# Host-laid taps and biases, an early load, a peeled last attention pair, and other memory for tiles of the triangle

## The chip, the cores and the metric

The kernel runs on one core of a Trainium2 chip, as one program. A core has TensorE (PE: matrix products into PSUM), VectorE (DVE), ScalarE (ACT), GpSimd (POOL) and SyncE (SP), each with its own stream of instructions, and 16 DMA engines that move data between DRAM and the on-chip memory (SBUF). The streams wait for each other by semaphores. The metric is the time of an execution on the device in microseconds (us), the median of several. Inputs may be laid out anew on the host; arithmetic on them is done by the kernel.

## The reference

An image x of 256 x 256 pixels by 128 channels in 32-bit floats passes through four layers. Each adds its output to x, and each begins with a normalisation over 32 groups of channels (`_gn`).

```python
# layer 0: row-wise attention, 4 heads of 32
zn = layernorm(gn(x)); q, k, v = zn @ Wq, zn @ Wk, zn @ Wv
a = softmax(q k^T / sqrt(32) + zn @ Wb)
x = x + (sigmoid(zn @ Wg) * (a @ v)) @ Wo
# layer 1: 16 steps of a gated complex recurrence, h <- f * (A h) + inp
A, B = fft2(pad(7x7 taps)), with A scaled below 0.95
f = sigmoid(u @ Wf + bf + 2); inp = 0.1 softplus(u @ Wd + bd) * sigmoid(u @ Wi + bi) * (B u)
x = x + h16
# layer 2: triangle product
p = layernorm(gn(x)); left, right = sigmoid(p @ g_in) * (p @ p_in), halves
out = einsum('bikd,bjkd->bijd', left, right / L)
x = x + sigmoid(p @ g_out) * (layernorm(out) @ p_out)
# layer 3: 3x3 convolution with bias, then a 128x128 product
x = x + (conv(gn(x), kernel) + bias) @ W
```

## The kernel before

The program runs six stages, one after the other, and passes the image between them through DRAM. For most work of TensorE, VectorE and ScalarE the order is the order of the code (`keep_in_program_order`, often behind a short name `pin`). For the rest, above all for where a load stands in its queue, a scheduler decides. Tiles come from pools; a tile in a pool waits until the earlier user of the same slot (or, for a pool that is closed and whose memory is used again, of the same bytes) is done. SP issues the loads, one after the other: a load that must wait holds all that are queued behind it. GpSimd issues the stores and does a little arithmetic. The very first weights are loaded from ScalarE's queue.

1. *Statistics* (`statistics`, about 0 to 134 us). Sums for the first normalisation over 32 chunks of 1 MB of x: VectorE subtracts a shift (`xs`, L220), ScalarE squares, TensorE adds up. The last seven chunks stay in SBUF. Beside this, `attention_weights` (L274) loads the weights of the attention, the block matrix `m32` as the last of them, and `bounded` (L470) computes a bound for the scores; its VectorE operations stand ahead of the first `xs`, among them one that multiplies by `m32` (L492). `kernel_rows` (L165) brings the 7 x 7 taps into two tiles of 21 x 64 x 32 (`ka0`, `ka1`): two memsets (L176) and eight loads (L178), all on GpSimd. TensorE makes 16 row transforms from them, and GpSimd stores these in the DRAM tensor `HD_`.
2. *Layernorm and transposition* (`attention`, to about 455 us), over the same 32 chunks. At chunk 5 `later_weights` (L312) queues the weights of the later layers on SP, among them three biases of the recurrence, each by two loads.
3. *Attention* (`attend_bounded`, 465 to 1707 us), 128 pairs of rows, about 9.6 us each. For one pair: scores into PSUM (`sc`, two buffers of two banks), bias added (`e`, VectorE), exponential (ScalarE), the two key halves added up (`ks`, `fold`), 48 matmuls for numerators and denominators (`nd`, one buffer of two banks, `values`), then `dn` (`gated`), its inverse on ScalarE (`inverse`), the quotient `og` (`divide`), the product with `Wo` (`px`) and the residual `x` (`output`), and squares for the next normalisation. The inverse, quotient and output of a pair are done in the turn of the next pair; after the loop the last pair's follow.
4. *Recurrence* (`recurrence`, to 3239 us), 64 blocks. `load(0)` fetches, with the block of x, the row transforms `hs` of that block from `HD_` by eight small loads; TensorE makes the column transform `za` from it.
5. *Triangle* (`triangle`, L1049). First part: 32 chunks are normalised (`zc`, `zs`, `zn`) and stored in `znT`; the load of `xin` (L1119) runs two chunks ahead, and `zn` has three buffers in the pool "t1". Second part, four quarters of the channels: 128 steps of `z` from `zt` (a load of 1 MB at L1169 for every two steps; `zt` has five slots in the pool `zp`, which is open from the beginning of the first part), gate `sg`, product into `LR`; then 32 steps of `po`, scaled and stored to `prodD`. `prepare` (`transformed_taps`, L1284) then transforms the taps of the convolution: `kw` and helpers in the pool "cwt", ending on VectorE at L1318. Last part: 32 steps with `pe` from `zn`, `zc` from the product `pr`, the layernorm and the output product `py`; loads of `zn`, `pr` and `xin` at L1213.
6. *Convolution* (`convolution`, to the end), untouched by the diff.

Of the kernel before, what the change touches and what calls it, by code (L numbers as in the profile page):

```python
# [9 lines left out]
F32 = mybir.dt.float32  # L10
# [7 lines left out]
P = 128  # L18
N = 256
# [3 lines left out]
KS = 7  # L23
HC = P // 2
# [6 lines left out]
class Kernel:  # L31
# [133 lines left out]
    def kernel_rows(self, sp, ps, HD_):  # L165

        nc, I = self.nc, self.i
        CG = HC // 4  # L170
        tu = self.load(sp, I["c_rows"], "tu")
        H, ka = [], []
        for n, (re, im) in enumerate((("A_real", "A_imag"), ("B_real", "B_imag"))):
            kr, ki = (I["L1_conv_" + y].rearrange("c p q -> p c q") for y in (re, im))
            k = sp.tile([3 * KS, HC, 32], F32, name=f"ka{n}")
            nc.gpsimd.memset(k, 0.0)  # L176
            for p0, q0, src in ((0, 0, kr), (0, KS, ki), (KS, 0, ki), (2 * KS, KS, kr)):
                nc.gpsimd.dma_start(k[p0:p0 + KS, :, q0:q0 + KS], src)  # L178
            ka.append(k)

        pin = lambda f: lambda *a, **k: self.tc.keep_in_program_order(f(*a, **k))

        def spectrum(g):
            n, g0 = divmod(2 * g, CG)
            if not g0:
                H.append(sp.tile([P, N, CG], F32, name="H", bufs=2))
            ph = ps.tile([P, 2, N], F32, name="ph", bufs=2)
            for j in range(2):
                for k in range(4):
                    pin(self.mm)(ph[32 * k:32 * k + 32, j], ka[n][:, CG * k + g0 + j, :], tu)  # L190
            pin(nc.scalar.copy)(H[n][:, :, g0:g0 + 2].rearrange("q u c -> q c u"), ph)
            if g0 + 2 == CG:
                for k in range(4):
                    nc.gpsimd.dma_start(HD_[n, :, k], H[n][32 * k:32 * k + 2 * KS])
        return spectrum
# [116 lines left out]
    def later_weights(self, pool):  # L312

        nc, I = self.nc, self.i
        W = self.weights = {}
        for g in "fid":
            W["W" + g] = self.load(pool, I["L1_conv_W" + g], "rw" + g)
            W["b" + g] = pool.tile([P, 2], F32, name="rb" + g)
            for half in range(2):
                with nc.allow_non_contiguous_dma("a bias vector"):  # L320
                    nc.sync.dma_start(W["b" + g][half * HC:(half + 1) * HC], I["L1_conv_b" + g].rearrange("(r c) -> c r", c=HC))

        W["ev"] = pool.tile([P, 2 * N], F32, name="ev")
        for o in range(0, P, 32):
            nc.sync.dma_start(W["ev"][o:o + 2 * KS], I["c_cols"])
        for n in ("in_w", "in_b", "out_w", "out_b"):
            W[n] = self.column(pool, I["L2_conv_ln_" + n], "ln2" + n)
        for n, src in (("p", "L2_p_in"), ("g", "L2_g_in"), ("o", "L2_p_out"), ("e", "L2_g_out"), ("kt", "L3_kernel"), ("wd", "L3_conv_W")):
            W[n] = self.load(pool, I[src], "w2" + n)
        W["bv"] = self.column(pool, I["L3_conv_bias"], "bv")  # L330

    def attention(self, wp, later, xT, x1T, znT, biasD, HD_, stats1, shift1):
        nc, tc, I = self.nc, self.tc, self.i
# [4 lines left out]
        with ExitStack() as c:  # L338
# [103 lines left out]
            for m in range(NM):  # L442
                turn(m + 1)
                variance(m)
                centre(m + 1, 0)
                normalise(m)
                pair_bias(m - 1)
                centre(m + 1, 1)
                if m == 5:
                    self.later_weights(later)  # L450
                elif m == NM - 4:
                    load_bias(0, 192)
                    nc.sync.dma_start(first[0], znT[:, :1024])
                    nc.sync.dma_start(first[1], xT[:, :1024])
                elif m == NM - 1:
                    load_bias(192, 240)
# [79 lines left out]
    def attend_bounded(self, xT, x1T, znT, bias, first, w, wo, stats1, shift1):  # L536


        nc, tc = self.nc, self.tc
        V = nc.vector  # L540
        with ExitStack() as c:
# [86 lines left out]
            def values(rp):  # L628

                v = t[rp, "v"]  # L630
                nd[rp] = ps.tile([P, 2, 2, N], F32, name="nd", bufs=1)
                for r in range(2):
                    i = 2 * rp + r
                    for kc in range(2):
                        for h in range(NH):
                            hs = slice(h * HD, (h + 1) * HD)
                            mm(nd[rp][hs, r, 0], v[:, 2 * r + kc, hs], es[i][:, h, kc], start=kc == 0, stop=kc == 1)
                    for h in range(NH):
                        mm(nd[rp][h * HD:(h + 1) * HD, r, 1], ones, ks[i][:, h])
# [51 lines left out]
            for i in range(2):  # L691
                score(i)
                for p2 in range(2):
                    biased(i, p2)
                    exponent(i, p2)
            for rp in range(N // 2):
                a, b = 2 * rp, 2 * rp + 1
                score(a + 2)
                inverse(rp - 1)
                biased(a + 2, 0)  # L700
                biased(a + 2, 1)
                divide(rp - 1)
                for nm in "qkvg":
                    if nm == "g":
                        exponent(a + 2, 0)
                    project(rp + 2, nm)
                fold(a)
                fold(b)
                output(rp - 1)
                score(b + 2)  # L710
                exponent(a + 2, 1)
                squares(rp - 1)
                for p2 in range(2):
                    biased(b + 2, p2)
                    exponent(b + 2, p2)
                values(rp)
                gated(rp)
            inverse(N // 2 - 1)
            divide(N // 2 - 1)
            output(N // 2 - 1)  # L720
            squares(N // 2 - 1)

    def attend_any(self, xT, x1T, znT, bias, w, wo, stats1, shift1):

# [88 lines left out]
    def recurrence(self, x1T, x2T, HD_, stats1, shift1, stats2, shift2):  # L813
# [7 lines left out]
        with ExitStack() as c:  # L821
# [44 lines left out]
            def load(b):  # L866
                d = D[b]
                xf = d["xf"] = io.tile([P, 1024], F32, name="xf", bufs=4)
                nc.sync.dma_start(xf, x1T[:, b * 1024:(b + 1) * 1024])
                xc = d["xc"] = io.tile([P, 2, 512], F32, name="xc")  # L870
                for half in range(2):
                    src = x1T[:, b * 1024 + half * 512:b * 1024 + (half + 1) * 512]
                    nc.sync.dma_start(xc[half * HC:(half + 1) * HC], src.rearrange("(r c) n -> c r n", c=HC))
                hs = d["hs"] = io.tile([P, 2, HC], F32, name="hs")
                for n in range(2):
                    for r in range(2):
                        o = 64 * n + 32 * r
                        for j in range(2):
                            nc.sync.dma_start(hs[o:o + 2 * KS, j].rearrange("q (k c) -> q k c", k=4),
                                              HD_[n, :, :, b * 4 + r + 2 * j, :])  # L880

# [165 lines left out]
    def triangle(self, x2T, x3T, znT, prodD, stats2, shift2, stats3, prepare):  # L1049
# [12 lines left out]
        with ExitStack() as c:  # L1062
# [47 lines left out]
            with ExitStack() as c1:  # L1110
# [31 lines left out]
                for m in range(NB // 2):  # L1142
                    load(m + 2)
                    centre(m + 1, 0)
                    rs = variance(ps, work, [sq[m, b] for b in range(2)])
                    square(m + 1, 0)
                    centre(m + 1, 1)
                    square(m + 1, 1)
                    pr = spreads(ps, rs)
                    zn = io.tile([P, 2048], F32, name="zn")  # L1150
                    for b in range(2):
                        z = zn[:, b * 1024:(b + 1) * 1024]
                        tt(z, zs[m, b], pr[b], MUL)
                        nc.gpsimd.tensor_scalar(z, z, lnw, lnb, MUL, ADD)
                    nc.gpsimd.dma_start(znT[:, m * 2048:(m + 1) * 2048], zn)

            with ExitStack() as c1:
# [6 lines left out]
                for g in range(G):  # L1164

                    for b in range(NB):
                        if b % 2 == 0:
                            zt = zp.tile([P, 2048], F32, name="zt")
                            nc.sync.dma_start(zt, znT[:, b * 1024:(b + 2) * 1024])  # L1169
                        z = ps.tile([P, 8, P], F32, name="z", bufs=3)  # L1170
                        for ch in range(8):
# [112 lines left out]
    def transformed_taps(self, late, kt, wd, bv):  # L1284
# [7 lines left out]
        MUL, ADD, SUB = ALU.mult, ALU.add, ALU.subtract  # L1292
        with ExitStack() as c:
            ps = c.enter_context(self.pool(name="cwp", bufs=2, space=PSUM))
            wt = c.enter_context(self.pool(name="cwt", bufs=1))
            pb = ps.tile([P, 2], F32, name="cpb")
            self.mm(pb[:, 0:1], wd, bv)
            V.tensor_copy(bw, pb[:, 0:1])
# [225 lines left out]
def arrays_of(inputs):  # L1524


    arrays = constants()
    for name, a in inputs.items():
        a = np.asarray(a)
        if name in _RENAMED:  # L1530
            if name == "L3_conv_kernel":
                a = a.reshape(9, P, P).transpose(2, 0, 1)
            else:
                a = a.T
            name = _RENAMED[name]
        arrays[name] = np.ascontiguousarray(a)
    return arrays


# [14 lines left out]
```

## Time and profile before

| what | us |
|---|---|
| three runs: median (lowest, highest) | 5127.24 (5122.95, 5130.06) |
| profiled execution | 5126.96 |
| its span | 5125.2 |
| busy: TensorE, VectorE, ScalarE, GpSimd | 4948.5, 4100.7, 3496.2, 414.2 |
| idle of TensorE ahead of the first `pe` of the triangle's last part | 9.82 |
| start of the first `xs` | 23.20 |
| last `og` and `x` of the attention | 1703.46, 1706.33 |

The times in the lower rows count from the start of the span. The profiled execution's own time is 1.8 us more than its span, which begins with the first and ends with the last recorded instruction. A line of a timeline or of a group of instructions is read so: start, busy time, engine, line of the kernel, operation, output <- inputs, shape, count, and in brackets the engine's idle time before it, with what ended it. "L60" is the line of the helper that issues every matmul and "L54" that of ScalarE's operations, so that these are told apart by the names of tiles. Waits of a DMA load appear where it stands in its queue (SPq). The granted clock of TensorE was 0.988 on average.

### The profile page before, as it was taken

What the parts mean: (1) busy time and instruction counts of PE and PEld (TensorE: products, weight loads), DVE (VectorE), ACT (ScalarE), POOL (GpSimd) and SP (SyncE); (2) the same over time, 40 slices, a digit from 0 to 9 for tenths busy, and PEclk for the clock granted to TensorE, in tenths of its full rate; (3) what the DMA queues carried; (4) which work ended last, traced back from release to release, by engine and by line L of the source; (5) the groups of instructions that cost most, each with busy time, mean ns of one, the idle gap of its engine ahead of it and who ended that gap; (6) DMA issues with size and microseconds to landing.
All of it is one profiled execution on the core that took longest, in us unless ns stands there. A gap on an engine that the chain in (4) does not pass through costs nothing.

```text
span 5125.2 us, 78589 instructions
## 1 busy us (share of the span) xinstructions
PE 4948.5 (97%) x31357; PEld 2702.7 (53%) x31357; DVE 4100.7 (80%) x4797; ACT 3496.2 (68%) x4948; POOL 414.2 (8%) x600
## 2 busy tenths in 40 slices
PE   7999999999999899999999999899999989989999
PEld 2444555555555333333333333229999953349999
DVE  6666999999999799999999999675333537779886
ACT  5445888888888799999999999453333357762110
POOL 1332000000000000000000000240111010000000
PEclk9999999999999899999999999999999999999999
DMA  8794222222222122222222222687666678865432
GB/s 282 277 338 186 83 79 87 83 80 87 83 80 82 59 76 63 76 63 76 63 76 63 76 63 67 253 304 280 239 229 238 237 277 325 327 224 188 140 121 67
DMA packets 205054, 781.44 MB, mean 152 GB/s; under 512 B 56857, under 2 KB 60263, under 8 KB 155423
## 3 DMA queue, kind: packets, MB, share of 16 engines
q1 hardware_dynamic: 147070, 505.57, 29.3%
q0 software_dynamic: 56320, 270.42, 14.5%
q8 instruction: 250, 4.10, 0.3%
q14 instruction: 118, 0.96, 0.1%
q10 hardware_dynamic: 1296, 0.40, 0.0%
HBM read 504.94 MB, written 271.32 MB: 151 GB/s over the span
## 4 chain that ended last, share of the span: by engine, by line
PE 56%; DVE 28%; issue 5%; ACT 1%; DMA 1%; POOL 0%; POOLq 0%; DVEq 0%; SPq 0%; ACTq 0%
PE z L60 9%; PE m L60 7%; PE nd L60 7%; PE sc L60 5%; PE po L60 4%; PE zc L60 4%; DVE tr L896 3%; DVE t L893 3%; DVE y L893 3%; DVE p L893 3%; DVE yf L893 3%; PE ppq L60 3%; PE ppv L60 2%; PE px L60 2%; PE pe L60 2%
## 5 line engine op out<-in xcount | busy, mean ns | idle before, releaser
L559 DVE TENSOR_TENSOR e<-sc,bT 128x1024 f32<-128x1024 f32 x512 | 603.2, 1220 | 52.4 <-PE sc L60 51.2
L54 ACT ACTIVATE e<-e 128x1024 f32<-128x1024 f32 x512 | 540.5, 1056 | 63.0 <-DVE e L559 49.2
L1056 DVE TENSOR_TENSOR LR<-z,sg 128x512 f32<-128x512 f32 x256 | 268.2, 1049 | 365.0 <-ACT sg L54 365.0
L60 PE MATMUL m<-U,v 128*128 128x128 f32 x4608 | 517.6, 276 | 6.6 <-DVE v L1403 6.6
L60 PEld LDWEIGHTS m<-U,v 128*128 128x128 f32 x4608 | 517.4, 193 | 6.7 <-DVE v L1403 6.7
L60 PE MATMUL z<-wf,zt 128*128 128x128 f32 x4096 | 460.4, 276 | 2.1 <-DVE zn L1056 1.3
L60 PEld LDWEIGHTS z<-wf,zt 128*128 128x128 f32 x4096 | 460.0, 193 | 3.9 <-DVE zn L1056 2.8
L54 ACT ACTIVATE sg<-z 128x512 f32<-128x512 f32 x256 | 152.8, 597 | 309.9 <-PE z L60 308.0
L54 ACT ACTIVATE sq<-zs 128x1024 f32<-128x1024 f32 x192 | 202.4, 1054 | 196.4 <-DVE zs L370 156.8
L559 DVE TENSOR_TENSOR ks<-e 128x1024 f32<-128x1024 f32 x256 | 300.9, 1217 | 0.0
L60 PE MATMUL sc<-tq,tk 32*128 32x256 f32 x4096 | 298.2, 403 | 2.8 <-DVE e L559 1.9
L60 PE MATMUL nd<-e,tv 128*32 128x256 f32 x4096 | 272.0, 383 | 0.0
L60 PEld LDWEIGHTS sc<-tq,tk 32*128 32x128 f32 x4096 | 187.3, 185 | 160.5 <-issue 97.1
L54 ACT ACTIVATE dn<-dn 128x512 f32<-128x512 f32 x384 | 241.7, 629 | 13.3 <-DVE dn L559 2.6
L60 PE MATMUL av<-y,ident 128*128 128x512 f32 x384 | 191.3, 607 | 44.9 <-DVE y L893 44.9
L60 PE MATMUL po<-LR 128*128 128x256 f32 x1024 | 222.2, 380 | 6.9 <-DVE LR L1056 6.9
L1440 ACT COPY m4s<-m 128x512 f32<-128x512 f32 x32 | 18.7, 584 | 287.8 <-PE m L60 287.8
L60 PEld LDWEIGHTS po<-LR 128*128 128x128 f32 x1024 | 194.1, 190 | 34.2 <-DVE LR L1056 7.7
L60 PE MATMUL bx<-p,ident 128*128 128x512 f32 x384 | 193.3, 612 | 0.0
L54 ACT ACTIVATE o<-po 128x256 f32<-128x256 f32 x256 | 84.3, 381 | 145.4 <-issue 110.5
L60 PEld LDWEIGHTS nd<-e,tv 128*32 128x32 f32 x4096 | 120.3, 110 | 109.8 <-issue 44.2
L862 ACT ACT_TABLE_LOAD x132 | 169.4, 1283 | 1.6
(368 smaller groups left out, 10276.9 us busy)
## 6 DMA issues: line engine op xcount, KB each, us to landing
zt<-znT SPq DMA_DIRECT2D x128, 1024.0 KB
znT<-zn POOLq DMA_DIRECT2D x64, 1024.0 KB, 5.3
xin<-x2T SPq DMA_DIRECT2D x64, 1024.0 KB
xin<-in_x_dram SPq DMA_DIRECT2D x50, 1024.0 KB
xr<-x3T SPq DMA_DIRECT2D x46, 768.0 KB
xT<-xo POOLq DMA_DIRECT2D x32, 1024.0 KB, 9.2
xr<-xT SPq DMA_DIRECT2D x64, 512.0 KB
zn<-znT SPq DMA_DIRECT2D x64, 512.0 KB
```

What stands on the lines that cost most here:

```text
L54: return self.nc.scalar.activation(out, in_, func, bias=bias, scale=scale, **kw)
L60: return self.nc.tensor.matmul(out, lhsT, rhs, start=start, stop=stop)
L559: pin = lambda f: lambda *a, **k: tc.keep_in_program_order(f(*a, **k))
L862: pin(nc.scalar.preload_act_table_set(want))
L893: pin(V.tensor_tensor(out, a, b_, op))
L896: pin(V.scalar_tensor_tensor(out, a, k, b_, op0, op1))
L1056: pin = lambda f: lambda *a, **k: tc.keep_in_program_order(f(*a, **k))
L1440: nc.scalar.copy(m4, m[4])
```

## The change

The taps are put into the shape of the tiles `ka0` and `ka1` on the host, with the zeros, and the biases as 128 x 2; each is then one load. The eight loads of row transforms become a method, `row_transforms`; block 0 calls it at chunk 12 of the layernorm, into a tile of its own in the pool `later`. In the attention the last pair is taken out of the loop: its `nd` takes a slot of `sc`, and its matmuls stand ahead of the quotient and output of the pair before. In the triangle the first part's `zn` comes from `zp`, under the same five slots as `zt`. The pool "cwt" is allocated at the other end of SBUF.

```diff
@@ -170,12 +170,9 @@
         CG = HC // 4
         tu = self.load(sp, I["c_rows"], "tu")
         H, ka = [], []
-        for n, (re, im) in enumerate((("A_real", "A_imag"), ("B_real", "B_imag"))):
-            kr, ki = (I["L1_conv_" + y].rearrange("c p q -> p c q") for y in (re, im))
+        for n in range(2):
             k = sp.tile([3 * KS, HC, 32], F32, name=f"ka{n}")
-            nc.gpsimd.memset(k, 0.0)
-            for p0, q0, src in ((0, 0, kr), (0, KS, ki), (KS, 0, ki), (2 * KS, KS, kr)):
-                nc.gpsimd.dma_start(k[p0:p0 + KS, :, q0:q0 + KS], src)
+            nc.gpsimd.dma_start(k, I["L1_taps"][n])
             ka.append(k)
 
         pin = lambda f: lambda *a, **k: self.tc.keep_in_program_order(f(*a, **k))
@@ -315,10 +312,7 @@
         W = self.weights = {}
         for g in "fid":
             W["W" + g] = self.load(pool, I["L1_conv_W" + g], "rw" + g)
-            W["b" + g] = pool.tile([P, 2], F32, name="rb" + g)
-            for half in range(2):
-                with nc.allow_non_contiguous_dma("a bias vector"):
-                    nc.sync.dma_start(W["b" + g][half * HC:(half + 1) * HC], I["L1_conv_b" + g].rearrange("(r c) -> c r", c=HC))
+            W["b" + g] = self.load(pool, I["L1_b" + g], "rb" + g)
 
         W["ev"] = pool.tile([P, 2 * N], F32, name="ev")
         for o in range(0, P, 32):
@@ -328,6 +322,16 @@
         for n, src in (("p", "L2_p_in"), ("g", "L2_g_in"), ("o", "L2_p_out"), ("e", "L2_g_out"), ("kt", "L3_kernel"), ("wd", "L3_conv_W")):
             W[n] = self.load(pool, I[src], "w2" + n)
         W["bv"] = self.column(pool, I["L3_conv_bias"], "bv")
+
+    def row_transforms(self, t, HD_, b):
+
+        for n in range(2):
+            for r in range(2):
+                o = 64 * n + 32 * r
+                for j in range(2):
+                    self.nc.sync.dma_start(t[o:o + 2 * KS, j].rearrange("q (k c) -> q k c", k=4),
+                                           HD_[n, :, :, b * 4 + r + 2 * j, :])
+        return t
 
     def attention(self, wp, later, xT, x1T, znT, biasD, HD_, stats1, shift1):
         nc, tc, I = self.nc, self.tc, self.i
@@ -448,6 +452,8 @@
                 centre(m + 1, 1)
                 if m == 5:
                     self.later_weights(later)
+                elif m == 12:
+                    self.first_rows = self.row_transforms(later.tile([P, 2, HC], F32, name="hs0"), HD_, 0)
                 elif m == NM - 4:
                     load_bias(0, 192)
                     nc.sync.dma_start(first[0], znT[:, :1024])
@@ -628,7 +634,7 @@
             def values(rp):
 
                 v = t[rp, "v"]
-                nd[rp] = ps.tile([P, 2, 2, N], F32, name="nd", bufs=1)
+                nd[rp] = ps.tile([P, 2, 2, N], F32, name="nd", **({"tag": "sc"} if rp == N // 2 - 1 else {"bufs": 1}))
                 for r in range(2):
                     i = 2 * rp + r
                     for kc in range(2):
@@ -693,7 +699,7 @@
                 for p2 in range(2):
                     biased(i, p2)
                     exponent(i, p2)
-            for rp in range(N // 2):
+            for rp in range(N // 2 - 1):
                 a, b = 2 * rp, 2 * rp + 1
                 score(a + 2)
                 inverse(rp - 1)
@@ -715,10 +721,20 @@
                     exponent(b + 2, p2)
                 values(rp)
                 gated(rp)
-            inverse(N // 2 - 1)
-            divide(N // 2 - 1)
-            output(N // 2 - 1)
-            squares(N // 2 - 1)
+
+            rp = N // 2 - 1
+            inverse(rp - 1)
+            fold(N - 2)
+            fold(N - 1)
+            divide(rp - 1)
+            values(rp)
+            gated(rp)
+            output(rp - 1)
+            inverse(rp)
+            squares(rp - 1)
+            divide(rp)
+            output(rp)
+            squares(rp)
 
     def attend_any(self, xT, x1T, znT, bias, w, wo, stats1, shift1):
 
@@ -871,13 +887,7 @@
                 for half in range(2):
                     src = x1T[:, b * 1024 + half * 512:b * 1024 + (half + 1) * 512]
                     nc.sync.dma_start(xc[half * HC:(half + 1) * HC], src.rearrange("(r c) n -> c r n", c=HC))
-                hs = d["hs"] = io.tile([P, 2, HC], F32, name="hs")
-                for n in range(2):
-                    for r in range(2):
-                        o = 64 * n + 32 * r
-                        for j in range(2):
-                            nc.sync.dma_start(hs[o:o + 2 * KS, j].rearrange("q (k c) -> q k c", k=4),
-                                              HD_[n, :, :, b * 4 + r + 2 * j, :])
+                d["hs"] = self.first_rows if b == 0 else self.row_transforms(io.tile([P, 2, HC], F32, name="hs"), HD_, b)
 
 
 
@@ -1147,7 +1157,7 @@
                     centre(m + 1, 1)
                     square(m + 1, 1)
                     pr = spreads(ps, rs)
-                    zn = io.tile([P, 2048], F32, name="zn")
+                    zn = zp.tile([P, 2048], F32, name="zn", tag="zt")
                     for b in range(2):
                         z = zn[:, b * 1024:(b + 1) * 1024]
                         tt(z, zs[m, b], pr[b], MUL)
@@ -1165,7 +1175,7 @@
 
                     for b in range(NB):
                         if b % 2 == 0:
-                            zt = zp.tile([P, 2048], F32, name="zt")
+                            zt = zp.tile([P, 2048], F32, name="zt", tag="zt")
                             nc.sync.dma_start(zt, znT[:, b * 1024:(b + 2) * 1024])
                         z = ps.tile([P, 8, P], F32, name="z", bufs=3)
                         for ch in range(8):
@@ -1292,7 +1302,7 @@
         MUL, ADD, SUB = ALU.mult, ALU.add, ALU.subtract
         with ExitStack() as c:
             ps = c.enter_context(self.pool(name="cwp", bufs=2, space=PSUM))
-            wt = c.enter_context(self.pool(name="cwt", bufs=1))
+            wt = c.enter_context(self.pool(name="cwt", bufs=1, side="right"))
             pb = ps.tile([P, 2], F32, name="cpb")
             self.mm(pb[:, 0:1], wd, bv)
             V.tensor_copy(bw, pb[:, 0:1])
@@ -1534,6 +1544,16 @@
                 a = a.T
             name = _RENAMED[name]
         arrays[name] = np.ascontiguousarray(a)
+
+
+    taps = np.zeros((2, 3 * KS, HC, 32), np.float32)
+    for n, m in enumerate("AB"):
+        re, im = (arrays.pop(f"L1_conv_{m}_{y}").transpose(1, 0, 2) for y in ("real", "imag"))
+        for p0, q0, a in ((0, 0, re), (0, KS, im), (KS, 0, im), (2 * KS, KS, re)):
+            taps[n, p0:p0 + KS, :, q0:q0 + KS] = a
+    arrays["L1_taps"] = taps
+    for g in "fid":
+        arrays["L1_b" + g] = np.ascontiguousarray(np.tile(arrays.pop("L1_conv_b" + g).reshape(2, HC).T, (2, 1)))
     return arrays
```

## The prediction

> **What bounds the kernel now.** I read the page's engine and chain parts first, to learn who carries the end, and then five places in the trace where the edits act: the timeline of VectorE at the start, the windows of DMA traffic, TensorE's timeline at the end of the attention, the chain of work through the normalisation of the triangle, and the timelines at its two later borders.
>
> ```profile
> PE 4948.5 (97%) x31357; PEld 2702.7 (53%) x31357; DVE 4100.7 (80%) x4797; ACT 3496.2 (68%) x4948; POOL 414.2 (8%) x600
> ...
> PE 56%; DVE 28%; issue 5%; ACT 1%; DMA 1%; POOL 0%; POOLq 0%; DVEq 0%; SPq 0%; ACTq 0%
> ```
>
> TensorE is busy 97% of the span, and the chain that ends last runs on TensorE and VectorE. The edits remove no instruction from either, so they can win only idle time at a border. DMA is 1% of the chain, about 51 us; the question is which of these microseconds go.
>
> The start, VectorE's timeline (start, duration, instruction, idle before and its releaser):
>
> ```profile
> 15.91 0.23 DVE L300 TENSOR_SCALAR woh<-wo 128x128 f32<-128x128 f32 x1 [5.69 <-DMA wo<-in_L_conv_Wo_dram]
> ...
> 18.14 0.28 DVE L497 TENSOR_REDUCE sums<-jq 128x1 f32<-128x128 f32 x1
> 22.79 0.29 DVE L492 TENSOR_TENSOR junk<-junk,m 128x128 f32<-128x128 f32 x1 [4.37 <-DMA m<-in_c_block_dram]
> ...
> 23.20 2.35 DVE L220 TENSOR_TENSOR xs<-xin,sh 128x1024 f32<-128x1024 f32 x2
> ```
>
> The first chunk's `xs` stands behind `junk` (L492), which waits for the block matrix m32 to 22.79. The first chunk of x had landed long before. m32 was issued at 5.40 and `wo` at 4.91, both on ScalarE's queue; a weight issued at 3.58 landed 2.26 us later. The windows show why they took 10 and 17 us (columns: window, its length, busy time of PE, PEld, DVE, ACT, POOL, then granted clock, DMA share, GB/s):
>
> ```profile
> 5.00:10.00 5.00, 2.89 (x12) 2.32 (x12) 2.63 (x15) 1.28 (x1) 5.00 (x7) 1.00 0.96 248
> 10.00:15.00 5.00, 1.14 (x4) 0.84 (x4) 0.22 (x2) 0.00 (x0) 0.96 (x2) 1.00 1.15 141
> 15.00:20.00 5.00, 1.77 (x6) 1.43 (x6) 1.87 (x9) 0.00 (x0) 0.00 (x0) 1.00 1.01 95
> ```
>
> ```profile
> 4165.00:4185.00 20.00, 16.96 (x54) 6.00 (x53) 6.33 (x6) 14.62 (x16) 0.00 (x0) 1.00 1.01 419
> ```
>
> From 10 to 20 us the DMA engines are as full as at 4165, but move 95 to 141 GB/s instead of 419. In this time GpSimd's eight tap loads are in flight (issued 4.24 to 10.16, the last landing at 24.1), 12.2 KB each in runs of 7 floats.
>
> The end of the attention, TensorE's timeline:
>
> ```profile
> 1695.84 1.33 PE L60 MATMUL px<-og,wo 128*128 128x512 f32 x2 [2.88 <-DVE og L559]
> 1697.09 1.94 PE L60 MATMUL nd<-e,tv 128*32 128x256 f32 x16
> ...
> 1700.71 0.60 PE L60 MATMUL nd<-ks,ones 128*32 128x256 f32 x8
> 1704.21 2.08 PE L60 MATMUL px<-og,wo 128*128 128x512 f32 x2 [2.89 <-DVE og L559]
> ```
>
> `nd` of the last pair begins only after `og` of the pair before has read the one `nd` buffer.
>
> The triangle's normalisation, chain of work:
>
> ```profile
> 3286.26 8.95 DMA znT<-zn
> 3295.23 0.33 SPq L1169
> 3295.66 15.46 DMA xin<-x2T
> ```
>
> A store of zn holds a zt load (L1169) at SP's head, and the xin load queued behind it comes late. Chunks that otherwise start every 6.33 us then start at 3301.27, 3310.68 and 3317.42: 9.41 + 6.74 − 2 × 6.33 = 3.49 us lost.
>
> Border to the quarters (VectorE), then border to the last stage (the chain, then TensorE's timeline):
>
> ```profile
> 3464.45 2.81 DVE L1056 TENSOR_TENSOR LR<-z,sg 128x512 f32<-128x512 f32 x3 [6.19 <-ACT sg L54]
> ```
>
> ```profile
> 4153.63 0.48 DVE U L1318
> ...
> 4154.16 4.91 DMA zn<-znT
> ```
>
> ```profile
> 4147.83 1.55 PE L60 MATMUL cpk<-w2wd,w2kt 128*128 128x128 f32 x11
> 4159.20 6.28 PE L60 MATMUL pe<-zn,w2e 128*128 128x512 f32 x8 [9.82 <-DMA zn<-znT]
> ```
>
> LR is first written at 3464.45, although its `sg` was ready at 3461.61: the memory is that of the last zn, whose store landed at 3464.08. The last stage's first zn lies over kw, so its load leaves only when L1318 is done, and TensorE idles 9.82 us.
>
> **What the Trainium skill says.** "DMA: Bandwidth & Descriptors", section Specifications: line rate wants transfers of at least 512 B. The trace agrees in direction (28 B runs, 95 to 141 GB/s). The same page, "Issuing engines are not separate DMA queues": transfers of SP, ScalarE and GpSimd run on the same 16 engines and interleave; agreed, since the taps stretch ScalarE's 64 KB load from 2.26 to 17 us. "TensorE: Matmul & The Clock Gate", "What's actually happening": an idle window of about 3.4 us halves the clock; agreed, `pe` takes 6.28 us after 9.82 idle and 3.63 afterwards.
>
> **Part by part.**
>
> *Taps (A).* Removed: two memsets (3.54 us of GpSimd) and eight loads; added: two loads of 172 KB in 8 KB runs, issued near 1 us. The 246 KB more cost about 1.0 us at 248 GB/s. With the slow traffic gone, x's first two chunks at 360 GB/s (the rate around 8 us) are in by about 12, and `wo` and m32 between them by about 10 to 11.5. From `wo`'s first use to L492 being ready to run are 18.42 − 15.91 = 2.5 us, so the first `xs` starts near 13.2 against 23.20: gain 10.0. Ends: 13 if everything lands in 2.3 us (then the first chunk, landed 10.69, decides), 2.5 if x's own traffic is what delays m32. I take 10: the slow packets begin and end with the taps. From the first `xs` the stage goes as before (TensorE fills 25 to 30 us), so the gain travels.
>
> *Biases and early hs (B).* On SP three loads for six, and eight hs loads moved from the recurrence's first block to the layernorm, in two lots of four between later weights and chunks of x. The eight took 1707.76 to 1715.05, 7.3 us of SP's queue; the chunks behind them are needed 40 us later or more, which hides it. In the recurrence TensorE goes from zd straight to za at 1717.11 without waiting for hs: gain 0. Without that cover it would cost 7.3.
>
> *Last pair (C).* nd in a scores' buffer starts when its last e exists, 1693.0. The two `ks` move ahead of og(126) and end at 1696.05. nd's 48 matmuls end near 1696.9; then dn 0.7, ScalarE 2 × 0.64, x(126) 0.7 in between, og 0.65, px 1.33 from 1699.7 (2.08 if cold), x at about 1701.5 against 1706.33. og(126) and px(126) go behind nd, where TensorE would otherwise idle; ScalarE's squares(126) goes behind the last inverse, and nobody waits for it. Gain 4.8 (4.4 to 5.3).
>
> *zn in zt's slots (D).* The five early zt loads leave their places among the xin loads, so SP no longer stalls on a store: gain 3.5 (3 to 4). The price: zt 0 to 3 now wait for the stores of zn 27 to 30, landing 3439.5 to 3458.5, and land about 5 us later; they are needed at 3457.2 and each 3.57 us from about 3463. All come ahead by my count, the closest by 2 to 3 us.
>
> *LR free of zn (E).* LR can start at 3461.6, 2.8 earlier. But TensorE runs z ahead in three PSUM buffers and idles only 0.76 at 3464.77: gain 0.8 (0 to 2).
>
> *kw elsewhere (F).* zn(0) and most of pr(0) load during the quarters' po matmuls. `pe` then waits for bwc alone (done 4150.56): 4150.6 to 4154.2 at 3.63 warm. The last rows of pr follow the last product's store (issued 4148.03), landing near 4153. So zc(0) starts at about 4154.3 against 4165.49: gain 11.2. Limit: from 4165 to 4185 the DMA runs at 419 GB/s; pr(1) would land near 4160.8 and is needed at 4164. If that slips, the gain is 8, at worst 7; at best 13.
>
> Sum: 10.0 + 0 + 4.8 + 3.5 + 0.8 + 11.2 = 30.3. The profiled execution took 5126.96 us (span 5125.2, the rest lies around it), 0.3 below the median of 5127.24: 5096.7, or 5097 on the median.
>
> **Rivals.**
>
> *Start bound by x itself.* Five chunks of 1 MB go out before 30 us and could fill the engines without any taps. For: at 5 to 10 us the share is 0.96. Against: that is at 248 GB/s and the slow time starts with the taps. A is 2.5, the time 5104.5.
>
> *Last stage fed by DMA.* For: shares of 0.90 to 1.01 from 4165 to 4225. Against: TensorE has no idle there from 4185. F is 8 or 7: 5100 to 5101.
>
> *Slower: first quarter starved.* Before, five zt stand ready when z starts; after, the quarter begins with one or two, and four of the five slots turn over at first. A slot gives four periods of 3.57 us = 14.3 us from release to landing. It decides from 4.5 us per MB (233 GB/s): 32 loads × 0.93 = 30 us, the whole gain; at 5 us per MB it costs 46: 5143. Against: other quarters hold 1 MB per 3.57 us (293 GB/s) with the same five slots, and VectorE's normalisation is over by then.
>
> *Hardly any change.* The same mechanism near its threshold, so that it eats 20 to 40 us: 5117 to 5137.
>
> **How the numbers follow.** Forecast 0.60 (own range 5091 to 5102), start bound by x 0.14, last stage fed by DMA 0.14, still faster than the forecast 0.02, hardly any change 0.06, slower 0.04. About 0.2%, 10.3 us, is what a measurement of this kernel tells from no change. The first four cases are all beyond it: faster 0.90, same 0.06, slower 0.04. High end: all lower ends, 2.5 + 4.4 + 3 + 0 + 7 = 16.9, 5110. Low end: all upper ends, 13 + 5.3 + 4 + 2 + 13 = 37.3, less 3 for the spread of runs: 5087.
>
> **What would show it.** A: first `xs` at 12 to 14, m32 landing before it, no window at 95 GB/s. C: the last `x` of the attention 4.8 earlier relative to the last scores. D: all chunks every 6.33 us, no zt load among xin. E: LR at about 4.3 us after z starts. F: `pe` about 1.2 us after cpk and 3.63 us long, zc 5 us after cpk. I would be wrong if zt loads showed up as what z waits for in the first quarter, if m32 still landed after 20, or if the last stage's first ten steps took over 12.99 us each for waiting on pr.

## The result and the profile after

| | median, us | lowest to highest | ratio to before, 95% interval |
|---|---|---|---|
| kernel before, beside it | 5126.1 (4 runs) | 5122.95 to 5130.06 | |
| changed kernel | 5095.51 (4 runs) | 5095.07 to 5096.92 | 0.994, 0.9923 to 0.9958 |
| changed kernel in a second set of runs (`e5_changed_again`) | 5095.01 (4 runs) | 5094.51 to 5099.2 | 0.9946, 0.993 to 0.9963 |

The changed kernel is about 30 us faster. Its profiled execution took 5096.92 us with a span of 5095.1. Where the 30.1 us of span went is read by taking the same instruction in both traces and noting how much earlier it starts. In the table, the last column is what each stretch added.

| up to | before | after | earlier by | added |
|---|---|---|---|---|
| first `xs` | 23.20 | 15.29 | 7.9 | 7.9 |
| third `e` of the attention (bias added, VectorE) | 468.82 | 460.37 | 8.45 | 0.5 |
| `tv` of the third pair (ScalarE) | 478.51 | 469.01 | 9.5 | 1.05 |
| last scores of the attention | 1688.43 | 1678.98 | 9.45 | 0 |
| last `x` of the attention | 1706.33 | 1692.53 | 13.8 | 4.3 |
| first `zc` of the triangle | 3243.56 | 3229.59 | 14.0 | 0.2 |
| a chunk after the late loads (`zc`) | 3317.56 | 3300.07 | 17.5 | 3.5 |
| first `LR` | 3464.45 | 3444.05 | 20.4 | see below |
| first `zc` of the last part | 4165.32 | 4135.63 | 29.7 | |

LR itself gained more than its border was worth, since TensorE had run ahead in its three buffers: from the fourth `sg` of ScalarE on, the same instruction is 18.5 us earlier, so the border added 1.0. From there to the first `zc` of the last part it is 11.2, and 0.4 more come until the end.

The start, VectorE's timeline of the changed kernel (start, duration, instruction, idle before and releaser):

```profile
12.47 0.23 DVE L297 TENSOR_SCALAR woh<-wo 128x128 f32<-128x128 f32 x1 [1.07 <-DMA wo<-in_L_conv_Wo_dram]
...
14.89 0.28 DVE L498 TENSOR_TENSOR junk<-junk,m 128x128 f32<-128x128 f32 x1
...
15.29 2.35 DVE L217 TENSOR_TENSOR xs<-xin,sh 128x1024 f32<-128x1024 f32 x2
```

The bracket behind `junk` is gone: m32 is there, and what `xs` now waits for is VectorE's own chain of small operations, held up once more by `wo`, which landed at 12.4. The windows of the changed kernel (columns as before):

```profile
5.00:10.00 5.00, 2.93 (x10) 2.50 (x10) 2.11 (x11) 1.28 (x1) 0.00 (x0) 1.00 0.92 275
10.00:15.00 5.00, 3.18 (x12) 2.48 (x12) 2.67 (x16) 0.00 (x0) 0.00 (x0) 1.00 1.00 363
15.00:20.00 5.00, 3.44 (x6) 0.49 (x6) 5.00 (x11) 2.32 (x3) 0.00 (x0) 1.00 0.44 128
```

From 10 to 15 us full engines now move 363 GB/s and not 141. The 128 of the third window belong to a share of 0.44: here the engines were not full.

The end of the attention, TensorE's timeline, first the last scores of the kernel before:

```profile
1688.43 1.80 PE L60 MATMUL sc<-tq,tk 32*128 32x256 f32 x16
```

Then the changed kernel:

```profile
1678.98 2.09 PE L60 MATMUL sc<-tq,tk 32*128 32x256 f32 x16
...
1687.00 1.05 PE L60 MATMUL nd<-e,tv 128*32 128x256 f32 x16
1687.87 0.61 PE L60 MATMUL nd<-ks,ones 128*32 128x256 f32 x8
1688.41 1.13 PE L60 MATMUL px<-og,wo 128*128 128x512 f32 x2
1691.37 1.13 PE L60 MATMUL px<-og,wo 128*128 128x512 f32 x2 [1.83 <-DVE og L565]
```

Both `px` follow the last `nd`, the second in 1.13 us where it took 2.08. From the start of the last scores to the last `x` are 13.55 us, before 17.90. (The 17.8 and 1.73 that the expectations and the profile's chain of work give count the scores from 1688.50, the end of the `px` ahead of them.)

The triangle's normalisation, TensorE's timeline of the changed kernel, and SP's at its end:

```profile
3293.74 1.98 PE L60 MATMUL zc<-xin,lc 128*128 128x512 f32 x4 [0.36 <-DVE zs L1066]
...
3300.07 1.98 PE L60 MATMUL zc<-xin,lc 128*128 128x512 f32 x4 [0.36 <-DVE zs L1066]
...
3306.40 1.99 PE L60 MATMUL zc<-xin,lc 128*128 128x512 f32 x4 [0.36 <-DVE zs L1066]
```

```profile
3412.60 0.32 SPq L1129 DMA_DIRECT2D xin<-x2T  x1
3422.21 0.34 SPq L1179 DMA_DIRECT2D zt<-znT  x1
```

The steps are 6.33 us, also where 9.41 had stood, and the first zt leaves after the last xin. The borders, VectorE's and then TensorE's timeline:

```profile
3444.05 1.05 DVE L1066 TENSOR_TENSOR LR<-z,sg 128x512 f32<-128x512 f32 x1 [3.37 <-ACT sg L54]
```

```profile
4128.45 2.42 PE L60 MATMUL cpk<-w2wd,w2kt 128*128 128x128 f32 x18
4132.10 3.70 PE L60 MATMUL pe<-zn,w2e 128*128 128x512 f32 x8 [1.23 <-DVE bwc L1308]
4135.63 3.60 PE L60 MATMUL zc<-pr,cmat 128*128 128x512 f32 x8
```

LR is released by `sg`, 4.4 us after z began (3439.61). `pe` waits 1.23 us for bwc, and `zc` follows it at once.

### The profile page after: what moved, and what is told of

It is laid out like the page before. It is cut to its first block, busy times and chain, and to the rows that moved or that the text cites. A ratio compares the mean times of both kernels' runs of the same rounds, so it can differ in the third digit from the quotient of the medians.

```text
span 5095.1 us, 78580 instructions
## 1 busy us (share of the span) xinstructions
PE 4938.7 (97%) x31357; PEld 2699.4 (53%) x31357; DVE 4100.7 (80%) x4797; ACT 3497.2 (69%) x4948; POOL 406.9 (8%) x592
## 5 line engine op out<-in xcount | busy, mean ns | idle before, releaser
L54 ACT ACTIVATE xp<-xr,ab 128x1536 f32<-128x1536 f32 (+1 forms) x48 | 76.9, 1653 | 137.6 <-DVE tf L1425 126.7
```

Of the source, the lines that this page charges most:

```text
L54: return self.nc.scalar.activation(out, in_, func, bias=bias, scale=scale, **kw)
```

## The experiments

**One part alone, four times** (12 to 20 executions each, on one chip, beside the kernel before at 5123.69; a gain in us is worked out from the ratio).

`e1_taps` is the kernel before with the first part of the diff.

```diff
-            nc.gpsimd.memset(k, 0.0)
-            for p0, q0, src in ((0, 0, kr), (0, KS, ki), (KS, 0, ki), (2 * KS, KS, kr)):
-                nc.gpsimd.dma_start(k[p0:p0 + KS, :, q0:q0 + KS], src)
+            nc.gpsimd.dma_start(k, I["L1_taps"][n])
...
+            W["b" + g] = self.load(pool, I["L1_b" + g], "rb" + g)
...
```

> The kernel before with only the taps and biases laid out on the host. Theory (the eight tap loads in runs of 28 B slow all DMA from 9 to 22 us, so wo and m32 come late): the first xs starts at 15.3 us as in the changed kernel, and every later stage runs 7.5 to 9.5 us earlier than before, so about 5117.5. Rival (x's own traffic delays m32): first xs not before 20, gain at most 3. In either case the end of the attention, the triangle's normalisation and the start of its last part keep the idle times they had before (9.8 us ahead of the first pe).

Measured: 5116.07 us, ratio 0.9983 (0.9977 to 0.999), 8.7 us of gain with an interval from 5.1 to 11.8. First `xs` at 15.35. The biases were not tried apart from the taps. The other borders still lose their time: 16.63 us from the last scores to the last `x`, 3.4 in the triangle's chunks, and 10.23 ahead of the first `pe`:

```profile
4132.99 2.42 PE L60 MATMUL cpk<-w2wd,w2kt 128*128 128x128 f32 x18
4145.64 5.86 PE L60 MATMUL pe<-zn,w2e 128*128 128x512 f32 x8 [10.23 <-DMA zn<-znT]
```

`e2_peel` takes the last pair out of the loop and does nothing else.

```diff
-                nd[rp] = ps.tile([P, 2, 2, N], F32, name="nd", bufs=1)
+                nd[rp] = ps.tile([P, 2, 2, N], F32, name="nd", **({"tag": "sc"} if rp == N // 2 - 1 else {"bufs": 1}))
...
-            for rp in range(N // 2):
+            for rp in range(N // 2 - 1):
...
+            values(rp)
+            gated(rp)
+            output(rp - 1)
```

> The kernel before with only the last attention pair taken out of the loop, its nd in a scores' buffer. Theory: from the start of the last scores to the last x 13.5 us where the kernel before takes 17.8; gain 4.3, about 5122, nothing else moves. Rival (the 4 us came from an earlier or warmer TensorE and not from the order): 17 us again and no gain.

Measured: 5121.39 us, ratio 0.9992 (0.9983 to 1.0001), which alone doesn't tell it from no change. The trace does: the last scores start at 1690.52 and the last `x` at 1704.08, 13.56 us apart, although these scores took 2.09 us and the kernel before's 1.80. This edit changes the buffer and the order together; which of the two would do alone was not tried.

`e3_zn_slots` moves zn alone.

```diff
-                    zn = io.tile([P, 2048], F32, name="zn")
+                    zn = zp.tile([P, 2048], F32, name="zn", tag="zt")
...
-                            zt = zp.tile([P, 2048], F32, name="zt")
+                            zt = zp.tile([P, 2048], F32, name="zt", tag="zt")
```

> The kernel before with only the normalisation's zn in zt's slots. Theory (a zt load that waits for a store holds the xin loads behind it at SP): no gap between chunks, gain 3.5 to 3.8 in the normalisation, and 0.8 more at the first LR, which no longer waits for the last store of zn: 4.3 to 4.6 in all, about 5122. The first pe still waits 9.8 us. Rival (the late xin came from a full DMA, not from SP's queue): the gap stays, gain at most 0.8.

Measured: 5118.11 us, ratio 0.9987 (0.9981 to 0.9994), 6.7 us. Chunks start at 3287.89, 3294.22, 3300.56 and 3306.89, every 6.33 us. By the trace the normalisation added 3.5 and LR 1.0; that is 4.5, inside the interval of the runs (3.1 to 9.7). The profiled execution was 7.2 us early before the triangle began, 3.9 of them at the start, which this edit doesn't touch; more on this below. A chunk in TensorE's timeline, then LR in VectorE's:

```profile
3306.89 1.98 PE L60 MATMUL zc<-xin,lc 128*128 128x512 f32 x4 [0.37 <-DVE zs L1056]
```

```profile
3450.88 1.05 DVE L1056 TENSOR_TENSOR LR<-z,sg 128x512 f32<-128x512 f32 x1 [3.37 <-ACT sg L54]
```

Its first `pe` still waits for zn, 10.17 us. A full DMA is not what made xin late.

`e4_right` moves kw's pool alone.

```diff
-            wt = c.enter_context(self.pool(name="cwt", bufs=1))
+            wt = c.enter_context(self.pool(name="cwt", bufs=1, side="right"))
```

> The kernel before with only the pool of kw at the other end of SBUF. Theory (the first zn of the last part lay over kw): zn and most of pr load during po, pe starts 1.2 us after cpk and takes 3.6 us, zc starts about 7 us after cpk where the kernel before takes 18; gain 11.4, about 5115. Rival 1 (the last part is fed by DMA): half of the gain is given back within its first six steps, 5 to 8 remain. Rival 2 (it needs zn's move as well): pe still waits 9.8 us.

Measured: 5111.51 us, ratio 0.9973 (0.9965 to 0.9981), 13.8 us with an interval from 9.7 to 17.9; by the trace 11.2 at this border. TensorE's timeline:

```profile
4146.19 2.42 PE L60 MATMUL cpk<-w2wd,w2kt 128*128 128x128 f32 x18
4149.84 3.70 PE L60 MATMUL pe<-zn,w2e 128*128 128x512 f32 x8 [1.23 <-DVE bwc L1298]
4153.37 3.60 PE L60 MATMUL zc<-pr,cmat 128*128 128x512 f32 x8
```

It doesn't need zn's move. From the start of cpk to the first `zc` are 7.18 us, as in the changed kernel; with kw in its old place it was 18.1 to 19.1 in four executions. Nothing is given back: through the last part TensorE waits for no load at all, in this kernel and in the changed one, although the DMA share is 0.93 to 1.01 in most of its first 80 us. These are all the longer waits of TensorE there in the changed kernel:

```profile
PE pr L60 <- ACT rs L54: 1.6, 1, 1.6
PE var L60 <- ACT sq L54: 1.4, 2, 0.9
PE pe L60 <- DVE bwc L1308: 1.2, 1, 1.2
```

**Do the parts add?** `e5_changed_again` is the changed kernel, on one chip with the next three.

> The changed kernel again, beside the three that follow, on one chip. The single parts came to about 8.7, 4, 6.7 and 13.8 us by their ratios, 33 in sum. Theory (the parts act at separate places and add): 0.9935 of the kernel before, 33 us less. Rival (two parts pay for the same idle time): less than 25.

Measured: 28.6 us by the medians (5123.6 to 5095.01); the ratio 0.9946 (0.993 to 0.9963) is 27.7 us, with an interval from 19 to 36. Like has to be compared with like: by their ratios the four single gains are 33.3 in sum, by their medians 7.6, 2.3, 5.6 and 12.2, which is 27.7. The runs alone therefore exclude neither the 33 nor the rival's 25. The traces decide: read from them, the parts are 7.9, 4.3, 3.5 + 1.0 and 11.2, 27.9 in sum, each at its own place and of the same size alone as together. No two pay for the same idle time.

**Why the taps cost what they did.** `e6_runs_128` keeps two loads of the same 344 KB, but cut into runs of 128 B.

```diff
-            nc.gpsimd.dma_start(k, I["L1_taps"][n])
+            nc.gpsimd.dma_start(k, I["L1_taps"][n].rearrange("c p q -> p c q"))
...
-    arrays["L1_taps"] = taps
+    arrays["L1_taps"] = np.ascontiguousarray(taps.transpose(0, 2, 1, 3))
```

> The changed kernel with its taps stored channel by channel, so that the same two loads read runs of 128 B (2,688 of them) where the changed kernel reads 8 KB. Theory (short runs are what slowed all DMA at the start): wo and m32 are late again, first xs at 19 to 22 us, 4 to 6 us slower than the changed kernel. Rival (the number of loads, eight, and the two memsets ahead of them did it): first xs at 15.3 and no difference.

Measured: 5101.84 us, ratio 0.9958 (0.9941 to 0.9974), 6.8 above the changed kernel's median with overlapping intervals. VectorE's timeline and the windows:

```profile
17.70 0.28 DVE L498 TENSOR_TENSOR junk<-junk,m 128x128 f32<-128x128 f32 x1
...
18.10 1.22 DVE L217 TENSOR_TENSOR xs<-xin,sh 128x1024 f32<-128x1024 f32 x1
```

```profile
5.00:10.00 5.00, 1.55 (x5) 1.21 (x6) 0.99 (x7) 1.28 (x1) 0.00 (x0) 1.00 0.98 163
```

A share of 0.98 moves 163 GB/s where the changed kernel moves 275, and the first `xs` is 2.8 us later. So neither the memsets nor the number of loads is needed; short runs do it. I had expected 4 to 6; I take the difference to be that the loads are issued earlier here, so that their slow time is over at 12.7. Of the 6.1 us that this profiled execution is longer than that of `e5_changed_again`, 2.9 are there before the last part begins, and 3.0 were lost in the last part to a TensorE at half clock, which is not the taps' doing (see the last section).

`e10_taps_after_x` and `e11_all_taps_late` leave the taps as they were in the kernel before, and hold the loads back. First `e10_taps_after_x`:

```diff
             nc.gpsimd.memset(k, 0.0)
+            nc.gpsimd.tensor_copy(k[:1, 0, :1], xin[:1, 0, :1])
+            nc.gpsimd.tensor_copy(k[:1, 0, KS:KS + 1], xin[:1, 0, :1])
...
```

> The kernel before with the same eight tap loads, held back on GpSimd until the second chunk of x has landed (a copy of one element from it into each tap tile ahead of the loads, overwritten by them). Theory (they slow whatever is in flight beside them): wo, m32 and x's first chunks land as in the changed kernel, first xs at 14 to 16 us; the loads then stretch x's next chunks for 13 us, and VectorE waits there for 3 to 8 us. Rival (the loads are slow only because the weights are in their way): first xs at 15 and nothing waits later.

Measured (one execution, 5121.03 us beside 5122.14): the copy touches only the rows of four of the eight loads, so the other four left at once, at 4.24 to 6.89, and four at 18.61 to 20.99. First `xs` at 18.75, which is 4.5 us earlier than before, and 4.2 of it were left at the end of the statistics. So this was half a dose. It says little: another execution of the kernel before started its first `xs` at 19.35 (below).

Then `e11_all_taps_late`:

```diff
             nc.gpsimd.memset(k, 0.0)
+            nc.gpsimd.tensor_scalar_mul(k[:, 0, :1], xin[:3 * KS, 0, :1], 0.0)
+            nc.gpsimd.tensor_scalar_mul(k[:, 0, KS:KS + 1], xin[:3 * KS, 0, :1], 0.0)
...
```

> The run before held back only four of the eight loads, those that overwrite the copied element; here zeros worked out from the second chunk of x are written where each of the eight will land, so all eight wait for that chunk. With eight loads early the first xs started at 23.2 us, with four at 18.75, with none (host layout) at 15.3. Theory (delay follows the loads in flight): 14.5 to 15.5 us here, and then waits of 3 to 8 us for x's next chunks, so that at most 6 us of the 8 are kept. Rival (memsets or the number of loads): 18 or later.

Measured: 5123.58 us, ratio 0.9999 (0.999 to 1.0007). GpSimd issued all eight at 15.68 to 21.49. VectorE's timeline and the windows:

```profile
12.75 0.28 DVE L494 TENSOR_TENSOR junk<-junk,m 128x128 f32<-128x128 f32 x1
13.15 2.35 DVE L222 TENSOR_TENSOR xs<-xin,sh 128x1024 f32<-128x1024 f32 x2
...
31.80 2.36 DVE L222 TENSOR_TENSOR xs<-xin,sh 128x1024 f32<-128x1024 f32 x2 [3.03 <-DMA xin<-in_x_dram]
```

```profile
20.00:25.00 5.00, 2.55 (x23) 0.63 (x19) 1.56 (x3) 2.61 (x4) 2.29 (x3) 1.00 1.03 86
25.00:30.00 5.00, 4.21 (x32) 0.57 (x29) 3.70 (x6) 4.17 (x4) 0.00 (x0) 1.00 1.22 166
```

The same eight loads carry their slow time with them: 86 GB/s at full engines now stands at 20 to 25 us. The first `xs` is 10.0 us earlier than before, and by 100 us all but 1.0 of it is given back, to x's chunks that come late and to a TensorE at half clock around 35 to 40 us (granted clock 0.50 in that window, before 0.73). I had expected that up to 6 us are kept; the trace kept 1.0, and the runs show no difference. So holding the same loads back gains next to nothing, and what the new layout gains comes from the shape of the taps.

**Taps behind the weights.** `e7_taps_last` puts the two loads on ScalarE's queue behind m32.

```diff
-            nc.gpsimd.dma_start(k, I["L1_taps"][n])
+            nc.scalar.dma_start(k, I["L1_taps"][n])
...
+                    next(weights)
                     spectrum = self.kernel_rows(sp, ps, HD_)
-                    next(weights)
```

> The changed kernel with the two tap loads on ScalarE's queue behind m32, where the changed kernel issues them on GpSimd's queue at once. Theory (A came 2 us short because 344 KB of taps now go ahead of the attention's weights): rawq lands 1.2 us earlier, wo and m32 1 to 2 us earlier, first xs at 13 to 14 us, 1 to 2 us faster than the changed kernel. Rival (x's own two chunks delay wo): first xs at 15 and no difference, or slower if the row transforms, whose taps come later, hold TensorE.

Measured: 5096.81 us (5092.94 to 5098.17), ratio 0.9949 (0.9933 to 0.9966), no difference to the changed kernel that these runs could show. In VectorE's timeline rawq's first use comes 1.1 us earlier than in the changed kernel's first profiled execution, `wo`'s 0.8 and the first `xs` 0.8, at 14.51:

```profile
11.70 0.23 DVE L297 TENSOR_SCALAR woh<-wo 128x128 f32<-128x128 f32 x1 [1.73 <-DMA wo<-in_L_conv_Wo_dram]
```

The direction is right and the size half of what was expected. `wo` still comes at 11.7, although by the DMA packets the taps moved only from 11.9 on; in `e11_all_taps_late` it was used at 10.14. What holds it here is not shown, and the rival, x's own chunks, is not excluded for this part.

**The early row transforms.** `e8_late_rows` loads them in the recurrence again.

```diff
-                elif m == 12:
-                    self.first_rows = self.row_transforms(later.tile([P, 2, HC], F32, name="hs0"), HD_, 0)
...
-                d["hs"] = self.first_rows if b == 0 else self.row_transforms(io.tile([P, 2, HC], F32, name="hs"), HD_, b)
+                d["hs"] = self.row_transforms(io.tile([P, 2, HC], F32, name="hs"), HD_, b)
```

> The changed kernel with the row transforms of block 0 loaded in the recurrence again. Theory (the eight loads are issued before TensorE wants them): no difference, within 1 us. Rival (za waits for them): up to 7.3 us slower, all of it between the last x of the attention and the first za.

Measured: 5099.82 us, ratio 0.9955 (0.9939 to 0.9972), 4.8 above the changed kernel's median with overlapping intervals. At the disputed place there is nothing: from the last `x` to the first `za` are 10.96 us, in the changed kernel 10.76, and `za` stands straight behind zd. The profiled execution, 4.5 us longer, lost its time elsewhere. The last chunks of the statistics come 4.1 us later, after a wait of VectorE for x at 86.06 (7.72 us, in the changed kernel 6.09 at 83.72); all but 1.3 of this is won back before the last part. There 3.0 us are lost where TensorE ran at half clock. First the changed kernel, then this one, both TensorE's timeline:

```profile
4145.45 3.70 PE L60 MATMUL zc<-pr,cmat 128*128 128x512 f32 x8
```

```profile
4147.69 5.72 PE L60 MATMUL zc<-pr,cmat 128*128 128x512 f32 x8
```

That the hs loads have no part in these two losses is argued from their place and was not tried; the rival's 7.3 us at `za` are excluded.

**How near is the first quarter to starving?** `e9_three_slots` leaves zn and zt three shared slots.

```diff
-            zp = quarters.enter_context(self.pool(name="tz", bufs=5))
+            zp = quarters.enter_context(self.pool(name="tz", bufs=3))
```

> The changed kernel with three shared slots for zn and zt where it has five; LR lies 16 KB lower by it, so the last part's first pr must wait for po and that border is not compared. Theory (a zt lands within about 5 us of its slot's release, two periods of 3.57 us are enough): after a late start of some 5 us in the first quarter, TensorE never waits for zt and a quarter's z stay at 114.4 us. Rival (the quarters' loads are near their limit): each z step waits for zt, a quarter's z takes 120 us or more.

Measured (one execution, 5106.15 us beside 5122.14 of the kernel before), the waits of TensorE through the first quarter:

```profile
PE z L60 <- DMA zt<-znT: 6.3, 2, 4.2
```

Two waits at the very start, 6.3 us together, and then none over 0.2 us to the end of the four quarters. (A quarter has 64 steps of `z`, not the 128 that the description of the kernel gives, and so 32 loads.) With five slots the changed kernel has no wait for zt there at all: a wide margin.

## Why the prediction was right

The forecast was 5097, and 5095.5 and 5095.0 were measured; the working gave a gain of 30.3, and 30.6 and 28.6 were measured. The mechanism was right at every border. The sum is better than its terms, though, and for that part it was luck.

- *Taps (A), 10.0 expected, 7.9 found.* The cause was right: `e6_runs_128` and `e11_all_taps_late` tie the late weights to short runs in flight. Mis-sized are the landing of `wo`, "about 10 to 11.5", and the way from there. The working priced the 246 KB more at 1.0 us and then didn't add it. The two loads now go ahead of the attention's weights: rawq's first use comes at 5.83 and not 4.62, m32 is issued 2.1 us later, and `wo` lands at 12.4. With the taps behind the weights (`e7_taps_last`) 0.8 of the missing 2.1 us come back. Another 0.4 is the step from L492 to `xs` (22.79 to 23.20 before), which the working leaves out. The last 0.9 stays open: `wo` lands at 11.7 even in `e7_taps_last`.
- There is also a floor that the working didn't see: VectorE's own chain of small operations, from rawq to `xs`. In `e11_all_taps_late` it runs from 4.57 to 13.15 with only 1.2 us of waits for weights, which is where the forecast's 13.2 was met; an upper end of 13 us, an `xs` at 10.2, would have left it no time. In `e5_changed_again` the chain alone decides. Rawq is first used at 6.47 and `xs` starts at 15.36, although VectorE doesn't wait for `wo`:

```profile
11.99 0.20 DVE L297 TENSOR_SCALAR woh<-wo 128x128 f32<-128x128 f32 x1
```

- The start of the kernel before varies from execution to execution. The same start gave a first `xs` at 23.20, 23.91, 19.35 and 24.27 in four profiled executions (before, `e2_peel`, `e3_zn_slots`, `e4_right`), and in five with the new taps 15.04 to 15.41. The gain of A is therefore 4 to 9 us, by which executions one compares.
- *Early hs (B), 0:* right at its place, by `e8_late_rows`; the eight loads had been ahead of `za` before too.
- *Last pair (C), 4.8 expected, 4.3 found,* in the changed kernel and alone. Two terms were off, in opposite directions. The working kept TensorE's clock of the kernel before; but the last scores took 2.09 us (1.80) and the first 16 matmuls of `nd` behind them 1.83 (1.07), so that the last dn starts 9.6 us after the scores where the working has 8.5. Then `x` follows the start of its px by 1.2 us where the working has 1.8. The clock also limits what 4.3 means: from the last scores to the last `x`, six executions with the old order took 16.3 to 17.9 us, and seven with the last pair taken out 11.8 to 13.9. The new order is faster in every one, by 2.4 to 6.1.
- *zn's slots (D), 3.5 expected, 3.5 found; LR (E), 0.8 expected, 1.0 found.* Both in `e3_zn_slots` alone, too. In four executions with zn in its own buffers the loss at the late loads was 3.4, 3.5, 3.5 and 5.9 us. LR comes 4.4 us after z starts, as said.
- *kw's place (F), 11.2 expected, 11.2 found,* all of it in `e4_right`, with `pe` 1.23 us behind cpk and 3.70 long.
- *What filled the gap that A left.* The working says nothing of it. In the attention's first pairs TensorE ran at half clock over a shorter stretch: from the `sc` that start at 467.62 (after: 459.54) to the `ppg` at 478.31 (468.81) it took 10.7 us before and 9.3 after, with the same instructions. One of them, first before, then after, in TensorE's timeline:

```profile
476.82 1.66 PE L60 MATMUL ppv<-rawv,zn 128*128 128x128 f32 x8
```

```profile
467.92 1.05 PE L60 MATMUL ppv<-rawv,zn 128*128 128x128 f32 x8
```

The same stretch took 9.0 to 10.7 us in ten other executions; 9.0 (`e11_all_taps_late`) and 10.7 (`e10_taps_after_x`) both stand in kernels with the attention of the kernel before. So it goes with the execution and not with the change. With some tenths at other borders and 0.4 at the end it made the sum come out.

Of the rivals, a start bound by x itself is excluded as the cause of the late m32 by `e11_all_taps_late` (x's first chunks in flight, and m32 there in time). A last part fed by DMA is excluded by TensorE's waits, which name no load. With three slots the first quarter waits 6.3 us at its start and then no more, with five not at all; so the slower case and the case of hardly any change had no ground.

## What to carry to other kernels

When a load is late, look in the windows for a full DMA share with few GB/s, and then for the load with short runs that is in flight beside it, even on another queue and with a small part of the bytes. Holding all of it back only moved the damage here; a layout with long runs removed it. A wait at a stage border is often one of memory and not of data: see what lay at the address before, or what stands ahead in the queue. Sums of small gains are checked best per place in the trace, in more than one execution where the clock has a part in them; the runs here showed 9 us clearly and could not tell 4 us from none.

## What the runs showed of the hardware that was not expected

- In the three cases at hand, the time over which loads with short runs slowed the others went with the number of runs and not with their bytes. By the DMA packets of the traces (the runs counted from the layout), 3,584 runs of 28 B (100 KB) took from 8.9 to 22.8 us in the kernel before, 3.9 ns for each, and from 19.8 to 32.2 in `e11_all_taps_late`, 3.5 ns; 2,688 runs of 128 B (344 KB) took from 3.8 to 12.7 in `e6_runs_128`, 3.3 ns. The same 344 KB in 42 runs of 8 KB took from 2.7 to 5.9.
- After the same instructions and the same idle of 1.61 us ahead of it, the same `pr` and `zc` of the last part ran at full clock in two executions of the changed kernel and in `e4_right` (1.14 and 3.70 us), at half clock in `e6_runs_128` and `e8_late_rows` (2.09 and 5.7), and partly so in `e7_taps_last` (2.04 and 4.45). That is up to 3.0 us, with nothing in the program to tell them apart at that place. The Trainium skill's "TensorE: Matmul & The Clock Gate", "What's actually happening", says that the window over which the clock judges is free-running; these six executions agree with that, and don't prove it.
